# A two-layer decoder on one core: weighted values in pairs, a bank of their own for the small transposes, a mask of rank 32, and an earlier schedule for latents, routing and expert blocks

## The chip, the core and the metric

The kernel runs on one core of a Trainium2 chip. The metric is device microseconds of one execution, the median of several runs. Five engines work side by side, each in the order of its own program: TensorE (PE in the profile, its weight loads PEld), VectorE (DVE), ScalarE (ACT), GpSimd (POOL) and SyncE (SP, which here only issues DMAs). An engine whose next instruction waits holds everything behind it on that engine.

## The reference

Everything is float32. `x` holds 32 sequences of 128 tokens with 128 features; `ctx` holds 32 x 128 tokens with 96 features. Six residual steps follow one another:

```python
x = x + L0_attn(ln(x))         # 16 heads of 8, rotation by position, softmax over all keys
x = x + L0_xattn(ln(x), ctx)   # 16 heads of 8, keys and values from ctx, scores clipped
x = x + L0_ffn(ln(x))          # 8 gated experts of width 64, best 2 of 8, and 2 shared ones
x = x + L1_attn(ln(x))         # 16 heads of 8, rotation by head, causal mask
x = x + L1_xattn(ctx, ln(x))   # "latents": 2 heads of 64, 128 context keys and 128 own, mask, unit-norm q and k
x = x + L1_ffn(ln(x))          # 8 experts of width 512, best 2 of 8:

probs = softmax(xf @ router_w + router_b);  topk_w, topk_i = top_k(probs, 2)
gates[token, topk_i] = topk_w / sum(topk_w)
h = relu(xf @ w1[e] + b1[e]);  y = h @ w2[e] + b2[e];  out = sum_e gates[:, e] * y_e
```

## The kernel before

**Slots.** A group is four sequences (`NG`), so there are eight groups (`G`). The three attention stages (`rope`, `cross`, `causal`) of 32 sequences each make 96 batches. Each batch takes two slots, one for each half of the heads (`h` = 0 in even slots, 1 in odd ones): slots 0 to 63 are rope, 64 to 127 cross, 128 to 191 causal. `attention` keeps a table `plan` of functions by slot and phase. In each slot it runs, in this order: phase `open`, phase `pre`, the slot's own score work, phase `inner`, the weighted values, phase `mid`, phase `post` (L543 to L621). This order is the program order of every engine. There is no other scheduler. `done(stage, g)` is the slot in which a group has left a stage: 8(8 stage + g) + 17.

**The slot's own work.** For slot k, four matmuls on 32 rows of the array give the scores of batch k//2 (two banks of `ps_s`), in two row groups; in between stand eight matmuls on the other two row groups, which give the transposed scores of the slot five earlier (`LAG`; two banks of `ps_t`). Both are L584. In the causal stage two bf16 matmuls (L553) of the whole 128 x 128 array, with 512 columns each, add the mask to the two score banks first. Then VectorE takes the maxima (L587), and ScalarE the exponentials of the transposed scores into two tiles `e` (L595), which GpSimd cuts to the causal triangle (L598). The weighted values (L612, 128 rows by 32 columns of the array) follow for the slot six earlier, half a batch in each slot; after the odd one ScalarE copies the bank `av` (the only bank of `ps_a`) to `sums` (L618).

**The small transposes.** Two slots after a batch began, phase `post`, the maxima are transposed (`max_pe`, L485), and VectorE makes `qa` of them in phase `pre` of the next slot (`max_out`, L493). Eight slots after, phase `post`, `sums` is transposed (`sums_pe`, L500), and in phase `pre` of the next slot VectorE divides by the totals (`sums_out`, L510, L511). Each transposition takes a bank of `ps_m`, a ring of three that all other stages share.

**Beside it.** The other steps stand in the same slots. Group g's gated experts begin at `done(1, g)`. Its latents begin at d = `done(2, g)` + 2: statistics, scales on GpSimd (L1036 to L1044), `turn`, `qkv` (d+4, d+5), norms (`square`, `total`, `root` as a power on GpSimd, L1089, in d+5 and d+6, `unit_heads` on VectorE, L953 to L955, in d+6 and d+7, phase `mid`), then four batches, one begun every two slots from d+8, each of four steps (`turn`, `score`, `turn_e`, `weigh`), then `leave` (d+18) and `project` (d+19). The router works on units of one or two groups, `UNITS`; each step (`scale`, `apply`, `turned`, `choice`, `choose2`, `choose3`, `ranks`) has a slot. Then each token's row goes to its expert's place in DRAM by an indirect DMA that GpSimd issues (`scatter`, L1679, eight a group, two a slot). The experts run in two halves (groups 0 to 3, and 4 to 7) of 23 blocks of 256 rows, one block a slot: SyncE fetches weights (`fetch_w`, L1809, four buffers) and rows (`fetch_x`, L1818), `turn` transposes (L1826), `hidden` (L1836, L1844, L1846) and `result` (L1853, L1861, L1863) compute, and `leave` writes the rows to their tokens with two indirect DMAs on GpSimd (L1868). The rows stand in tile `bo`, four buffers. At the end the two rows of each token are read back and added (`gather`, `finish`, L1881 to L1886). `begins` sets the slots: 209 and 234 for the two halves.

**Start.** GpSimd makes the constants (identity, masks) before its first layer-norm scale; the warm-up matmuls (L284) wait for `ident_b`.

Of the kernel before, what the change touches and what calls it, by code (L numbers as in the profile page):

```python
# [22 lines left out]
P = 128  # L23
# [85 lines left out]
def decoder(ctx: ExitStack, tc: tile.TileContext, a: dict, out: bass.AP):  # L109
# [115 lines left out]
    causal = cpool.tile([P, P], F32, tag="causal", name="causal")  # L225
    make_causal_mask(nc, causal, CAUSAL)
    causal_b = cpool.tile([P, P], BF16, tag="causal_b", name="causal_b")
    nc.gpsimd.tensor_copy(causal_b, causal)
# [28 lines left out]
    def attention(att, rope, stages, besides):  # L257
# [36 lines left out]
        batch = [dict() for _ in range(B * len(stages))]  # L294
        half = {}
# [181 lines left out]
        def plan_batch(bb):  # L477
# [5 lines left out]
            def max_pe():  # L483
                s["mp"] = bank(ps_m)
                nc.tensor.transpose(s["mp"][:, :P], msc, ident)  # L485
                if st.guard:
                    nc.gpsimd.tensor_copy(m_all[:, bb % B], strided_max(msc))

            def max_out():
                s["qa"] = att.tile([P, 2, P], F32, tag="qa", name="qa", bufs=3)  # L490

                for u in range(2):
                    nc.vector.scalar_tensor_tensor(  # L493
                        s["qa"][:, u, :], s["mp"][:, :P], head_rows[:, 1 - u : 2 - u], m["qz"][:, u, i * P : (i + 1) * P], ALU.mult, ALU.add
                    )

            def sums_pe():
                s["tp"] = bank(ps_m)
# [19 lines left out]
            at(t + 2, "post", max_pe)  # L518
            at(t + 3, "pre", max_out)
            at(t + LAG + 3, "post", sums_pe)  # L520
# [22 lines left out]
        for k in range(-max(LEADS.values()), final + 1):  # L543
            run(k, "open")
            run(k, "pre")
            if 0 <= k < last:
# [4 lines left out]
                if st.causal:  # L551
                    for j in range(2):
                        nc.tensor.matmul(  # L553
                            sc[j].rearrange("p (n k) -> p n k", n=4), ident_b, wide(causal_b, [P, 4, P], 1),
                            start=True, stop=False, skip_group_check=True,
                        )
# [33 lines left out]
            if two:  # L590
                st2 = stages[bb2 // B]
                half[k2] = []
                for j in range(2):
                    e = att.tile([P, 4, P], F32, tag="e", name="e", bufs=4)
# [9 lines left out]
            if 0 <= k3 < last:  # L604
                bb3, h3 = divmod(k3, 2)
                m3, i3, s3 = made[bb3 // NG], bb3 % NG, batch[bb3]
                if h3 == 0:
                    s3["av"] = bank(ps_a)
                es = half.pop(k3)
                for u in range(2):  # L610
                    for n in range(4):
                        nc.tensor.matmul(  # L612
                            s3["av"][32 * n : 32 * n + 32, h3 * P : (h3 + 1) * P], m3["vt"][:, i3, h3, n, u, :], es[u][:, n, :],
                            start=(h3 == 0 and u == 0), stop=(u == 1), skip_group_check=True,
                        )
                if h3 == 1:
                    s3["sums"] = att.tile([P, 2 * P], F32, tag="sums", name="sums")
                    nc.scalar.copy(s3["sums"], s3["av"][:, : 2 * P])  # L618
# [389 lines left out]
    def latent_attention(lazy, kv, row, bias, masked, plan_route):  # L1008
# [3 lines left out]

        def opened():
# [7 lines left out]
        def plan_group(at, g, d):  # L1021
            m = {}
# [77 lines left out]
            for u in range(2):  # L1100
# [3 lines left out]
                at(d + 6 + u, "mid", lambda u=u: unit_heads(flat(u), n4, m["nrm", u]))  # L1104
            for i in range(NG):
                plan_batch(at, m, g, i, d + 8 + 2 * i)
# [15 lines left out]
            at(d + 18, "mid", leave)  # L1122
            at(d + 19, "mid", project)
            plan_route(at, g, d + 19)

        def plan_batch(at, m, g, i, t):
            b, s = g * NG + i, {}

            def fetch():
                s["kv"] = opened().tile([P, KV], F32, tag="kv", name="lkv", bufs=3)  # L1130
# [37 lines left out]
            def weigh():  # L1168
                if i == 0:
                    m["on"] = opened().tile([P, NG, D], F32, tag="on", name="lon", bufs=1)  # L1170
# [21 lines left out]
        def beside(at, done):  # L1192
            for g in range(G):
                plan_group(at, g, done(2, g) + LATER)
# [331 lines left out]
    UNITS = [(0, 1), (2, 3), (4, 5), (6,), (7,)]  # L1526
    HALVES = [(0, 1), (2, 3, 4)]

    def router(slots, lazy):
# [8 lines left out]
        def plan_route(at, g, t):  # L1538
# [203 lines left out]

            for u in us:
                at(t + 1 - 8 * (us[-1] - u), "mid", stats(u, 0))
                at(t + 2 - 8 * (us[-1] - u), "pre", stats(u, 2))
            at(t + 2, "mid", scale)
            for u in us:
                at(t + 3 + u, "mid", apply(u, 0))
                at(t + 4 + u, "pre", apply(u, 2))
                at(t + 4 + u, "mid", turned(u))  # L1750
            t += us[-1]
            at(t + 5, "mid", choice)
            at(t + 6, "mid", choose2)
            if len(groups) > 1:
                t += 1
            at(t + 6, "mid", choose3)
            at(t + 7, "mid", ranks)
            n = 0
            for k in range(n2):
                for c in range(2):  # L1760
                    at(t + 8 + n // 2, ("pre", "inner")[n % 2], scatter(c, k))
                    n += 1
            for u in us:
                at(t + 8 + u, "mid", gates_over(u))
                at(t + 9 + u, "mid", bias(u))
# [3 lines left out]
    def expert_blocks(f, total, lazy):  # L1769
# [5 lines left out]
        def table():  # L1775

            def row(shape, tag, dtype=F32):
                return lazy["blocks"].tile([1] + shape, dtype, tag="tb_" + tag, name="tb_" + tag, bufs=2 if tag == "where" else 1)
# [69 lines left out]
        def result(j):  # L1848
# [8 lines left out]
            o = s["o"] = lazy["blocks"].tile([P, 2, D], F32, tag="o", name="bo", bufs=4)  # L1857
# [32 lines left out]
    def experts(halves, lazy, heads, late):  # L1890

        def beside(at, done):
# [4 lines left out]
            at(done(2, G - 1) + 2, "open", swap)  # L1897
            begins = [done(2, G // 2 - 1) + 40, done(2, G - 1) + 33]

            def plan_half(f):  # L1900
# [3 lines left out]
                for j in range(3):  # L1904
                    at(t - 3 + j, "post", lambda j=j: fetch_w(j))
# [218 lines left out]
```

## Time and profile before

| what | value |
|---|---|
| time, median of 3 runs | 1189.68 us (1186.5 to 1194.54) |
| the profiled execution | 1213.03 us, span 1211.2 us |
| PE busy | 1107.3 us, 91% of the span |
| DVE, ACT, POOL busy | 808.4, 572.9, 632.4 us |
| causal mask on PE, L553 | 128 matmuls, 40.9 us busy |
| weighted values on PE, L612 | 3072 matmuls, 126.5 us busy |
| indirect DMAs on POOL, L1868 and L1679 | 92 and 64, 997 ns each |

The busy time of PE counts a matmul from its start to a modelled end, so neighbours overlap and a busy PE is not one at its peak. fp32 matmuls appear twice, once a pass. The maxima (L587, two a slot) show where the slots lie in time: the rope stage takes about 28 us for eight slots, cross about 39, causal about 42; the last score slot, 191, ends near 865 us. Slots 192 to 209 follow without expert blocks; the first block's transposition (L1826, slot 210) starts at 947 us, that of the second half's first block (slot 235) at 1095 us, and the last block's results leave at 1188 us. Of these stretches the windows further down give the engines' busy times and the granted clock.

### The profile page before, as it was taken

What the parts mean: (1) busy time and instruction counts of PE and PEld (TensorE: products, weight loads), DVE (VectorE), ACT (ScalarE), POOL (GpSimd) and SP (SyncE); (2) the same over time, 40 slices, a digit from 0 to 9 for tenths busy, and PEclk for the clock granted to TensorE, in tenths of its full rate; (3) what the DMA queues carried; (4) which work ended last, traced back from release to release, by engine and by line L of the source; (5) the groups of instructions that cost most, each with busy time, mean ns of one, the idle gap of its engine ahead of it and who ended that gap; (6) DMA issues with size and microseconds to landing.
All of it is one profiled execution on the core that took longest, in us unless ns stands there. A gap on an engine that the chain in (4) does not pass through costs nothing. (4 is left out here: it accounts for less than half of the span.)

```text
span 1211.2 us, 30676 instructions
## 1 busy us (share of the span) xinstructions
PE 1107.3 (91%) x11923; PEld 818.1 (68%) x11923; DVE 808.4 (67%) x2290; ACT 572.9 (47%) x1302; POOL 632.4 (52%) x905
## 2 busy tenths in 40 slices
PE   8999999999999999999999999989988898888991
PEld 3576776676666676656666666666666688777991
DVE  4688888777877877677667678768666564353441
ACT  2355556666655555554445655644553432322330
POOL 3654555344345335434637664746747356664663
PEclk8899999999999999999999999989987898898996
DMA  7705333101021100111020000000102244445873
GB/s 201 240 22 178 99 99 99 54 28 37 3 45 45 46 21 18 37 37 37 2 50 2 11 15 14 15 10 28 32 19 98 93 141 129 145 142 161 256 227 107
DMA packets 83081, 92.09 MB, mean 76 GB/s; under 512 B 14274, under 2 KB 70264, under 8 KB 82928
## 3 DMA queue, kind: packets, MB, share of 16 engines
q1 hardware_dynamic: 77936, 81.57, 23.1%
q0 software_dynamic: 4992, 8.48, 2.0%
q8 instruction: 96, 1.57, 0.5%
q14 instruction: 57, 0.47, 0.1%
HBM read 53.84 MB, written 38.01 MB: 76 GB/s over the span
## 5 line engine op out<-in xcount | busy, mean ns | idle before, releaser
L595 ACT ACTIVATE e<-bank 128x512 f32<-128x512 f32 x384 | 208.1, 595 | 221.6 <-PE bank L584 213.6
L587 DVE TENSOR_REDUCE msc<-bank 128x4 f32<-128x512 f32 x384 | 245.8, 681 | 68.5 <-PE bank L584 67.0
L584 PE MATMUL bank<-kb,qz 32*128 32x256 f32 x1536 | 237.5, 412 | 7.8 <-DVE msc L587 6.1
L584 PE MATMUL bank<-qa,kb 32*128 32x128 f32 x3072 | 233.4, 288 | 1.6 <-ACT e L595 1.6
L584 PEld LDWEIGHTS bank<-qa,kb 32*128 32x128 f32 x3072 | 194.7, 190 | 4.5 <-ACT e L595 3.5
L584 PEld LDWEIGHTS bank<-kb,qz 32*128 32x128 f32 x1536 | 141.9, 189 | 78.8 <-issue 42.2
L1868 POOL DMA_INDIRECT y<-bo,bx x92 | 91.7, 997 | 87.7 <-ACT bo L1861 65.8
L612 PE MATMUL bank<-e,vt 128*32 128x128 f32 x3072 | 126.5, 282 | 2.4 <-POOL e L598 2.4
L598 POOL TENSOR_SCALAR_AFFINE_SELECT e<-e 128x512 f32<-128x512 f32 x128 | 79.1, 642 | 94.4 <-ACT e L595 94.2
L1853 PE MATMUL bank<-w,bh 128*128 128x128 f32 x736 | 95.4, 285 | 1.0 <-issue 0.9
L1853 PEld LDWEIGHTS bank<-w,bh 128*128 128x128 f32 x736 | 92.7, 201 | 4.8 <-issue 3.3
L1836 PE MATMUL bank<-bxT,w 128*128 128x256 f32 x368 | 93.0, 396 | 2.7 <-DVE bh L1846 1.0
L612 PEld LDWEIGHTS bank<-e,vt 128*32 128x32 f32 x3072 | 73.0, 110 | 27.8 <-POOL e L598 3.9
L1679 POOL DMA_INDIRECT slots<-rows,r_ati x64 | 63.8, 997 | 32.6 <-issue 16.5
L1836 PEld LDWEIGHTS bank<-bxT,w 128*128 128x128 f32 x368 | 69.9, 201 | 13.2 <-issue 2.0
L891 POOL TENSOR_TENSOR h<-h,g 128x512 f32<-128x512 f32 x30 | 37.6, 1271 | 71.5 <-DVE nm_st L798 44.8
L1846 DVE TENSOR_SCALAR bh<-bank,w 128x256 f32<-128x256 f32 x92 | 40.2, 478 | 43.9 <-PE bank L1836 35.1
L1861 ACT ACTIVATE bo<-bank,bx 128x128 f32<-128x128 f32 x46 | 16.9, 367 | 96.8 <-PE bank L1853 56.5
L323 ACT ACTIVATE xn<-x,ln_nb,ln_rs 128x128 f32<-128x128 f32 x96 | 42.1, 494 | 41.0 <-POOL ln_nb L317 41.0
L493 DVE SCALAR_TENSOR_TENSOR qa<-bank,head_rows,qz 128x128 f32<-128x128 f32 x192 | 57.6, 342 | 2.2 <-PE bank L485 2.2
L1844 ACT ACTIVATE bh<-bank,w 128x256 f32<-128x256 f32 x92 | 38.6, 471 | 40.1 <-PE bank L1836 15.1
L1157 ACT ACTIVATE le<-bank,lmx 128x256 f32<-128x256 f32 x64 | 26.9, 471 | 64.1 <-DVE lmx L1156 56.7
(322 smaller groups left out, 2280.9 us busy)
## 6 DMA issues: line engine op xcount, KB each, us to landing
w<-in_w_f SPq DMA_DIRECT2D x46, 514.0 KB
slots<-nowhere SPq DMA_DIRECT2D x8, 2340.0 KB
g<-spread SPq DMA_DIRECT2D x16, 512.0 KB
bx<-slots SPq DMA_DIRECT2D x46, 130.0 KB
kv<-kcv SPq DMA_DIRECT2D x8, 516.0 KB
lkv<-kv SPq DMA_DIRECT2D x32, 129.0 KB
y<-y SPq DMA_DIRECT2D x16, 256.0 KB
x<-in_x SPq DMA_DIRECT2D x8, 256.0 KB
```

The costliest lines, as they stand in the source:

```text
L323: nc.scalar.activation(m["xn"][:, i, :], X[g][:, i, :], AF.Identity, scale=m["rs"][:, i : i + 1], bias=m["nb"][:, i : i + 1])
L493: nc.vector.scalar_tensor_tensor(s["qa"][:, u, :], s["mp"][:, :P], head_rows[:, 1 - u : 2 - u], m["qz"][:, u, i * P : (i + 1) * P], ALU.mu ...
L584: nc.tensor.matmul(o, l, r, start=start, stop=stop, skip_group_check=True)
L587: nc.vector.tensor_reduce(tops(MSC[bb % 4], 2 * h + j), sc[j].rearrange("p (s n k) -> p s n k", s=2, n=2), AX.X, ALU.max, negate=True)
L595: nc.scalar.activation(e.rearrange("p n q -> p (n q)"), tr[j], AF.Exp, scale=SCALE)
L598: nc.gpsimd.affine_select(out=e, in_=e, compare_op=ALU.is_ge, fill=0.0, base=0, pattern=[[0, 4], [1, P]], channel_multiplier=-1)
L612: nc.tensor.matmul(s3["av"][32 * n : 32 * n + 32, h3 * P : (h3 + 1) * P], m3["vt"][:, i3, h3, n, u, :], es[u][:, n, :], start=(h3 == 0 and ...
L1679: ins = nc.gpsimd.indirect_dma_start(slots[f], bass.IndirectOffsetOnAxis(ap=m["ati"][:, c, n : n + 1], axis=0), m["rows"][c][:, n, :], Non ...
L1836: nc.tensor.matmul(ps[:, c * BLOCK : (c + 1) * BLOCK], s["w"][:, (2 * k + c) * P : (2 * k + c + 1) * P], s["xT"], start=True, stop=True,)
L1846: nc.vector.tensor_scalar(s["h"][:, n, :], p, bias, 0.0, ALU.add, ALU.max)
L1853: nc.tensor.matmul(ps[:, u * P : (u + 1) * P], s["h"][:, c, u * P : (u + 1) * P], s["w"][:, 512 + c * P : 512 + (c + 1) * P], start=(c == ...
L1868: ins = nc.gpsimd.indirect_dma_start(y, bass.IndirectOffsetOnAxis(ap=s["x"][:, u, D : D + 1].bitcast(U32), axis=0), s["o"][:, u, :], None, ...
```

## The change

1. **Weighted values in pairs.** Both halves of a batch now run together in the odd slot, 32 instructions in one go; the even slot has none. Tile `e` gets 6 buffers for 4.
2. **The transposes in their bank.** `max_pe` and `sums_pe` share one bank of `ps_a` and move from phase `post` to a new phase `turn`, ahead of `mid`, in the same (even) slot.
3. **The mask of rank 32.** Eight matmuls on 32 rows (128 columns each), in the row groups of the slot's scores, replace the two on 128 rows.
4. **Shorter chain.** `unit_heads` moves from `mid` to `pre` of its slot; the latents' batches begin at d+6, and for the last group at one slot's distance, with d two earlier. The router's steps stand half a slot apart; `UNITS` splits (4, 5). `lkv` gets 6 buffers for 3, `lon` 2 for 1.
5. **Sooner blocks.** `begins` becomes 203 and 226; the first half's weights are fetched one slot ahead; the small tables come from pool `route`; `bo` gets 6 buffers for 4.

```diff
+    causal_b = cpool.tile([P, 4, P], BF16, tag="causal_b", name="causal_b")
+    nc.gpsimd.memset(causal_b, 0.0)
+    ident_32 = cpool.tile([P, 32], BF16, tag="ident_32", name="ident_32")
+    for r in range(0, P, 32):
+        nc.gpsimd.affine_select(
+            out=causal_b[r : r + 32], in_=causal_b[r : r + 32], compare_op=ALU.is_ge, fill=CAUSAL, base=0,
+            pattern=[[-32, 4], [1, P]], channel_multiplier=-1,
+        )
+        nc.gpsimd.tensor_copy(ident_32[r : r + 32], ident[r : r + 32, r : r + 32])
...
             def max_pe():
-                s["mp"] = bank(ps_m)
-                nc.tensor.transpose(s["mp"][:, :P], msc, ident)
+                if t + 2 not in shared:
+                    shared[t + 2] = bank(ps_a)
+                s["mp"] = shared[t + 2][:, 2 * P : 3 * P]
+                nc.tensor.transpose(s["mp"], msc, ident)
...
             def sums_pe():
-                s["tp"] = bank(ps_m)
+                s["tp"] = shared[t + LAG + 3] = bank(ps_a)
...
-            at(t + 2, "post", max_pe)
+            at(t + LAG + 3, "turn", sums_pe)
+            at(t + 2, "turn", max_pe)
             at(t + 3, "pre", max_out)
-            at(t + LAG + 3, "post", sums_pe)
...
                 if st.causal:
-                    for j in range(2):
-                        nc.tensor.matmul(
-                            sc[j].rearrange("p (n k) -> p n k", n=4), ident_b, wide(causal_b, [P, 4, P], 1),
-                            start=True, stop=False, skip_group_check=True,
-                        )
+                    for c in range(4):
+                        for j in range(2):
+                            rows = slice(64 * h + 32 * j, 64 * h + 32 * j + 32)
+                            nc.tensor.matmul(
+                                sc[j].rearrange("p (n k) -> p n k", n=4)[:, :, 32 * c : 32 * c + 32], causal_b[rows, c, :],
+                                wide(ident_32[rows], [32, 4, 32], 1), start=(c == 0), stop=False, skip_group_check=True,
+                            )
...
-            if 0 <= k3 < last:
+            if 0 <= k3 < last and k3 % 2 == 1:
...
+                for h3 in range(2):
+                    es = half.pop(k3 - 1 + h3)
...
+            run(k, "turn")
...
+        steps = [2] * (G - 1) + [1]
...
-                at(d + 6 + u, "mid", lambda u=u: unit_heads(flat(u), n4, m["nrm", u]))
+                at(d + 6 + u, "pre", lambda u=u: unit_heads(flat(u), n4, m["nrm", u]))
             for i in range(NG):
-                plan_batch(at, m, g, i, d + 8 + 2 * i)
+                plan_batch(at, m, g, i, d + 6 + step * i)
...
-            at(d + 18, "mid", leave)
-            at(d + 19, "mid", project)
-            plan_route(at, g, d + 19)
+            end = d + 6 + step * (NG - 1) + 4
+            at(end, "mid", leave)
+            at(end + 1, "mid", project)
+            plan_route(at, g, end + 1)
...
-                plan_group(at, g, done(2, g) + LATER)
+                plan_group(at, g, done(2, g) + (LATER if steps[g] > 1 else 0))
...
-    UNITS = [(0, 1), (2, 3), (4, 5), (6,), (7,)]
-    HALVES = [(0, 1), (2, 3, 4)]
+    UNITS = [(0, 1), (2, 3), (4,), (5,), (6,), (7,)]
+    HALVES = [(0, 1), (2, 3, 4, 5)]
...
+            steps.append(scale)
+            for u in us:
+                steps += [apply(u, 0), apply(u, 2)]
+            steps += [turned(u) for u in us]
+            steps += [choice, choose2, choose3, ranks]
+            for n, fn in enumerate(steps):
+                at(t + 1 + (n + 1) // 2, ("mid", "pre")[n % 2], fn)
+            t += 1 + (len(steps) + 1) // 2
...
-            o = s["o"] = lazy["blocks"].tile([P, 2, D], F32, tag="o", name="bo", bufs=4)
+            o = s["o"] = lazy["blocks"].tile([P, 2, D], F32, tag="o", name="bo", bufs=6)
...
-            at(done(2, G - 1) + 2, "open", swap)
-            begins = [done(2, G // 2 - 1) + 40, done(2, G - 1) + 33]
+            at(done(2, G - 1) + 1, "open", swap)
+            begins = [done(2, G - 1) + 2, done(2, G - 1) + 2 + NB]
...
-                    at(t - 3 + j, "post", lambda j=j: fetch_w(j))
+                    at(t - 3 + j if f else t - 1, "post", lambda j=j: fetch_w(j))
```

## The prediction

> **What bounds the kernel now.** I read the page first, then busy time by stretch (rope, cross, causal, the slots after them, the first half's blocks, the change of halves, the second half's blocks, the end), then the groups by line, and the timelines of PE and DVE where a wait ended.
>
> ```profile
> core 0: us, PE busy (x) PEld busy (x) DVE busy (x) ACT busy (x) POOL busy (x), PEclk, DMA share, GB/s
> 25.00:275.00 250.00, 239.95 (x3233) 170.12 (x3231) 195.70 (x534) 135.70 (x300) 128.07 (x179) 0.97 0.34 105
> 275.00:526.00 251.00, 238.79 (x2970) 170.10 (x2970) 186.99 (x521) 141.02 (x298) 106.08 (x179) 0.99 0.13 30
> 526.00:865.00 339.00, 317.31 (x3681) 218.42 (x3681) 244.71 (x662) 177.11 (x409) 197.09 (x294) 0.97 0.09 22
> 865.00:947.00 82.00, 72.07 (x534) 52.03 (x532) 54.80 (x184) 39.91 (x105) 50.39 (x70) 0.87 0.19 58
> 947.00:1076.00 129.00, 119.09 (x775) 105.83 (x774) 67.07 (x242) 39.19 (x99) 70.39 (x86) 0.91 0.41 133
> 1076.00:1095.00 19.00, 11.23 (x74) 9.33 (x72) 4.42 (x11) 3.51 (x9) 11.89 (x13) 0.94 0.37 115
> 1095.00:1188.00 93.00, 89.40 (x598) 83.25 (x598) 38.67 (x97) 28.14 (x70) 52.69 (x51) 0.96 0.65 203
> ```
>
> In the three attention stages PE is busy 94 to 96%, DVE 72 to 78%: PE's order sets the pace, and DVE is near enough to stop it. From 865 to 1095 us PE is still busy, but at a clock of 0.87 to 0.94, and much of that is waiting in small pieces. In 1095 to 1188 it is full: 23 blocks, starting every 3.73 us. Nothing there changes.
>
> ```profile
> L612 PE MATMUL bank<-e,vt 128*32 128x128 f32 x3072 | 126.5, 282 | 2.4 <-POOL e L598 2.4
> L553 PE MATMUL bank<-causal_b,ident_b 128*128 128x512 bf16 x128 | 40.9, 395 | 1.4 <-DVE msc L587 1.3
> L485 PE MATMUL bank<-ident,msc 128*128 128x128 f32 x96 | 29.7, 309 | 16.9 <-DVE h L885 9.5 <-ACT le L1157 5.4 <-DVE h L886 1.9
> L500 PE MATMUL bank<-ident,sums 128*128 128x128 f32 x192 | 39.2, 286 | 3.2 <-ACT le L1157 2.2 <-DVE lon L1182 0.9
> ```
>
> The small transposes wait 16.9 and 3.2 us for a bank of the ring of three, held by a gated expert's tanh product or by the latents' exponential. One slot and one wait:
>
> ```profile
> 121.14 0.64 PE L612 MATMUL bank<-e,vt 128*32 128x128 f32 x16
> 121.71 0.44 PE L500 MATMUL bank<-ident,sums 128*128 128x128 f32 x2
> ...
> 700.72 0.33 PE L485 MATMUL bank<-ident,msc 128*128 128x128 f32 x1 [0.65 <-ACT le L1157]
> 700.89 0.59 PE L553 MATMUL bank<-causal_b,ident_b 128*128 128x512 bf16 x2
> 701.41 0.48 PE L584 MATMUL bank<-kb,qz 32*128 32x256 f32 x2
> ```
>
> Sixteen instructions of L612 hold PE 0.57 us from start to next start; the mask pair 0.52 us.
>
> **The change part by part** (signed us on the profiled execution's 1213.0, which lies 23 above the median; minus is gained).
>
> *Pairs, -17.* The starts of L612's sixteen lie 24 ns apart (0.64 us less one's 0.28, by 15), so 0.37 us, and 0.20 more pass before the next instruction. Two separate sets take 1.14 us, 32 in one go 31 x 0.024 + 0.20 = 0.95. 96 batches x 0.18 = 17.
>
> *Own bank, -20.* The 16.9 + 3.2 us above have no cause left: `ps_a` is emptied by the copy L618 a slot earlier. The ring's next user comes at least a score set (1.1 us) later.
>
> *The new wait, +24.* The paired L612 takes `ps_a` over from the transposes, so in every odd slot it waits until VectorE has done `max_out` and `sums_out` of that slot, and these stand behind all that VectorE has left of the slot before. Queued behind L612 is all of PE's `mid` and `post`. In the trace of before I laid each odd slot's start of L612 against the end of L493 and L511 in that slot: where these end later, the differences sum to 19 us in rope, 12 in cross, 10 in causal, 41 in all. The longest comes once in eight rope slots, 2.4 us:
>
> ```profile
> 123.74 0.64 PE L612 MATMUL bank<-e,vt 128*32 128x128 f32 x16
> 124.32 1.16 PE L441 MATMUL bank<-w_v,xT 128*128 128x128 f32 x8
> ```
> ```profile
> 124.02 0.17 DVE L953 TENSOR_SCALAR nrmc<-nrmc 128x8 f32<-128x8 f32 x1 [1.42 <-POOL nrmc L999]
> ...
> 125.56 0.60 DVE L493 SCALAR_TENSOR_TENSOR qa<-bank,head_rows,qz 128x128 f32<-128x128 f32 x2
> ```
>
> VectorE waits 1.42 us for a power on GpSimd, and `qa` is done at 126.16, after L612's 123.74. Part comes back: the next score set waits for the maxima anyway (about 1.1 us there). I take 60%, 24; bounds 0 and 41.
>
> *Mask, -10.* Per slot 0.52 us become eight matmuls of 128 columns in two row groups. The nearest row is L1145, two bf16 matmuls of 32 rows and 128 columns in one row group, whose starts lie 0.07 us apart, weights included. With the two groups side by side, four steps of 0.07, and 0.09 for the change of array shape that now stands ahead of the mask and not behind it: 0.37, so -0.15 x 64 = -10. A rule speaks against it: the Trainium skill, "TensorE: Matmul & The Clock Gate", Part 3, says that a weight load overlaps running matmuls only if it goes to another row group, and its section on LDWEIGHTS makes a load of 128 columns P/1.2, 107 ns. Then each group's step is 107 + 53 (128 columns at 2.4 GHz) = 0.16, the slot 0.64 + 0.09, and the mask would cost +13. The row shows 0.07 for a load and a matmul in one group, so I go by it. Bounds: L612's pace of 24 ns each (-15), the rule (+13).
>
> *`unit_heads` in `pre`, +10.* It now stands ahead of the maxima. In five groups the power of the second half (L1089) ends 1.8 us after the maxima of that slot began (group 0: 661.58 against 659.78), and the work itself is 1.3 us (0.30 + 0.20 + 0.83). VectorE blocks, the next score set is late by what PE's `mid` does not cover: 2 us a group, 10; bounds 0 and 16. It leaves `mid`, where it made one of the waits above.
>
> *Start, +3.* GpSimd cuts `causal_b` in four pieces of 512 columns ahead of `ident_b` and of its first scale. L598, the same shape, takes 0.64 us: 2.5 more, and copies. Warm-up and the first scale (5.49 us) move with it. Bounds 0 and 4.
>
> *Slots 192 to first block, -22.* 865 to 947 is 19 slots of 4.3 us, in which no engine is full: they are as long as their chains. Now 13, with more in each (latents of the last group one a slot): I take 4.6, 60 us for 82. Bounds -30 and 0.
>
> *First half's blocks to the second's, 0.* 947 to 1095 holds 25 slots and, in whole pieces, 119 us of PE work (23 x 3.73, the rest latents and routing); the same work, 120, falls into 23 slots. Removed: the stop at the change of halves,
>
> ```profile
> 1095.26 0.66 PE L1826 MATMUL bank<-ident,bx 128*128 128x128 f32 x2 [5.25 <-DMA bx<-slots]
> ```
>
> two blocks in 19 us, 11 too many, because rows are fetched after the last scatter. SyncE now also stands behind its third weight fetch, whose buffer (four) is freed by `result` of block 21 in slot 227, one slot after the row fetches were due: 4 remain, -7. And waits for a free `bo`:
>
> ```profile
> 1035.88 0.37 ACT L1861 ACTIVATE bo<-bank,bx 128x128 f32<-128x128 f32 x1 [5.20 <-remote]
> ```
>
> four of them, 22.5 us on ACT; L1853 right after runs at half clock (3.57 us for 1.79). Six buffers bear two more slots of lag: -6, though I can't see that every such wait is a buffer's. Added: with steps half a slot apart PE meets `turned` and `ranks` before POOL, ACT and DVE are done. A chain choose3 and gates is 2.6 us of VectorE against some 2 of PE: 3 us for each of three units, +9. In slots 217 to 223 GpSimd issues two scatters and two results a slot, 4 x 1.28 = 5.1 us against 3.7 to 5 of PE: it falls behind by some 7 us and takes 4 from PE, +4.
>
> *At no cost:* the sixth unit adds about 25 VectorE instructions of 0.2 us and one GpSimd power (1.05 us); VectorE is busy 67 of 129 us there and covers them, else 6 us. SyncE's fetches of context keys stand two slots earlier and its first three weight fetches one slot earlier each; it issues one in 0.9 us and has slots of 4 us. Buffers and the pool of the tables cost no instruction.
>
> Sum: -17 - 20 + 24 - 10 + 10 + 3 - 22 + 0 = -32, 1181 profiled, in the same proportion **1158** for the median.
>
> **The rivals.**
>
> *Slower: GpSimd behind its slots holds the router and PE with it.* Place: slots 205 to 223. `scale` is queued on GpSimd after results and scatters; `turned` on PE follows 1.5 slots later (two before) and nothing on PE passes it. From a lag of about 4 us on, each of three units stops PE for the rest (up to 12 us) and half clock for 3 more: +45, 1158 + 45 = 1203. For it: 65.8 us of POOL's waits are for `bo`, so it cannot run ahead; scatters of two units meet in slot 220. Against: POOL is busy 70 of 129 us.
>
> *The gain of the tail alone, or of attention alone, is returned.* If DVE's waits come back not at all (+17) and the mask serializes (+23), attention gives nothing, and with a tail of -10 the time is near 1185.
>
> *Better than forecast:* with DVE's waits absorbed (-24) and the mask at 24 ns (-5) 1130. That the mask's row groups do not run side by side, so that part 3 is no saving, is the +23 above.
>
> **How the numbers follow.** Forecast (1135 to 1177): 0.48. Absorbed waits (below 1135): 0.12. Gains returned (1178 to 1201): 0.18. Slower, by GpSimd: 0.22, half of it above 1210. One per cent is about what a measurement of this kernel tells from no change. So faster 0.60, same 0.18, slower 0.22; the range 1115 to 1210 leaves out the far half of the slower case and a little below.
>
> **What would show it.** Right: L485 and L500 without idle time; L612 with an idle time released by L493 or L511, about 24 us; the mask under 0.4 us a slot; the first L1826 some 30 us earlier or more; no idle of 5 us before the second half's. Wrong: mask starts 0.16 us apart; PE idle before L1591 or L1651 of over 4 us, released by POOL's `r_nb` or by the picks on DVE; halved clock through the first half's blocks.

## The result and the profile after

The changed kernel takes 1267.85 us (median of 4 runs, 1266.46 to 1272.2), the kernel before 1189.49 us beside it: ratio 1.066, interval 1.0616 to 1.0705. Forecast was 1158. It is slower by 78 us, more than any of the rivals had it.

The profiled execution of the kernel before that the prediction was worked on lay 23 us above its median. A second profile of it took 1191.86 us and differs only behind slot 191 (320.6 us for 341.1 up to the last addition on VectorE; the stages before agree within 1.2 us). So the losses are read here between that profile and one of the changed kernel on the same chip (1269.18 us). The stages are cut at the end of the second maximum on VectorE in slots 0, 64, 128 and 191, at the first block's transposes, and at the last addition on VectorE:

| us | before | changed | difference | forecast |
|---|---|---|---|---|
| start to slot 0 | 22.5 | 25.6 | +3.1 | +3 |
| rope | 224.2 | 248.8 | +24.6 | attention in all: -13 |
| cross | 279.6 | 300.0 | +20.4 | |
| causal | 338.6 | 351.1 | +12.5 | |
| slot 191 to the first block | 79.6 | 88.6 | +9.0 | -22 |
| first block to the end | 241.0 | 248.2 | +7.2 | 0 |

The page's groups of the changed kernel (lines have moved: L612 is L623 now, L485 is L494, L500 is L509, L493 is L502, the mask is L564; after the bar: busy us, mean ns of one, idle before it and what ended that):

```profile
L623 PE MATMUL bank<-e,vt 128*32 128x128 f32 x3072 | 118.0, 299 | 92.1 <-DVE qa L502 85.7 <-DVE on L520 2.2 <-POOL x L359 1.6
L509 PE MATMUL bank<-ident,sums 128*128 128x128 f32 x192 | 42.5, 304 | 0.0
L564 PE MATMUL bank<-ident,causal_b 32*128 32x128 bf16 x512 | 28.8, 223 | 12.9 <-DVE msc L598 12.7
L494 PE MATMUL bank<-ident,msc 128*128 128x128 f32 x96 | 26.4, 275 | 0.0
```

Two forecasts stand there: the small transposes have no idle time (16.9 and 3.2 us before), and the mask waits 12.7 us for maxima that stand behind `unit_heads` (+10 forecast). But L623 waits 92.1 us where L612 waited 2.4: 27 in rope, 35 in cross, 28 in causal, 2 behind. One of these waits, first on PE, then on DVE:

```profile
128.99 0.39 PE L595 MATMUL bank<-qa,kb 32*128 32x128 f32 x4
131.86 1.94 PE L623 MATMUL bank<-e,vt 128*32 128x128 f32 x32 [2.48 <-DVE qa L502]
```
```profile
126.90 1.26 DVE L598 TENSOR_REDUCE msc<-bank 128x4 f32<-128x512 f32 x2
129.57 0.17 DVE L964 TENSOR_SCALAR nrmc<-nrmc 128x8 f32<-128x8 f32 x1 [1.42 <-POOL nrmc L1010]
...
130.01 0.69 DVE L966 TENSOR_TENSOR kc<-kc,nrmc 128x512 f32<-128x512 f32 x1
130.62 0.25 DVE L519 RECIPROCAL rz<-bank 128x16 f32<-128x16 f32 x1
130.91 0.29 DVE L520 TENSOR_TENSOR on<-bank,rz 128x128 f32<-128x128 f32 x1
131.11 0.60 DVE L502 SCALAR_TENSOR_TENSOR qa<-bank,head_rows,qz 128x128 f32<-128x128 f32 x2
```

The bank's last reader, `qa`, ends at 131.71; VectorE came to it only after a power on GpSimd and a whole `unit_heads`, and L623 starts right behind. PE also comes back at half pace: these 32 matmuls take 1.94 us, those of an undisturbed slot 1.08; 21 of the 96 sets are slowed.

Busy time by stretch in the changed kernel (the columns after the engines: granted TensorE clock, DMA share, GB/s):

```profile
26.00:272.00 246.00, 213.81 (x2842) 159.84 (x2841) 175.60 (x474) 120.70 (x260) 116.50 (x158) 0.92 0.33 101
272.00:572.00 300.00, 263.48 (x3355) 194.26 (x3356) 205.18 (x583) 162.25 (x337) 116.67 (x200) 0.97 0.12 28
572.00:923.00 351.00, 303.38 (x4080) 230.61 (x4082) 242.87 (x676) 183.25 (x416) 201.23 (x300) 0.94 0.09 23
923.00:1012.00 89.00, 74.99 (x518) 58.39 (x508) 50.41 (x183) 33.59 (x86) 49.13 (x70) 0.71 0.16 48
```

Rope, cross and causal hold the same work as before but stretch, and their clock fell from 0.97, 0.99 and 0.97. Behind slot 191 there are 13 slots for 19, yet 89 us for 80, at 0.71 for 0.87.

### The profile page after: what moved, and what is told of

Its sections match the earlier page's. It is cut to its first block, busy times and chain, and to the rows that moved or that the text cites. A ratio compares the mean times of both kernels' runs of the same rounds, so it can differ in the third digit from the quotient of the medians.

```text
span 1265.1 us, 31429 instructions
## 1 busy us (share of the span) xinstructions
PE 1087.7 (86%) x12309; PEld 846.6 (67%) x12309; DVE 806.2 (64%) x2323; ACT 584.3 (46%) x1303; POOL 637.0 (50%) x917
## 4 chain that ended last, share of the span: by engine, by line
PE 48%; DVE 26%; POOL 11%; issue 8%; ACT 4%; DMA 2%; POOLq 0%; SPq 0%; DVEq 0%; ACTq 0%
PE bank L623 8%; PE bank L595 8%; DVE msc L598 4%; POOL y L1881 3%; PE bank L911 3%; DVE qa L502 3%; PE bank L378 2%; PE bank L1866 2%; PE bank L893 2%; PE bank L1849 2%; DVE h L897 2%; DVE on L520 2%; DVE h L896 2%; PE bank L415 2%; PE bank L1084 1%
## 5 line engine op out<-in xcount | busy, mean ns | idle before, releaser
L595 PE MATMUL bank<-qa,kb 32*128 32x128 f32 x3072 | 236.8, 293 | 1.8 <-ACT e L606 1.8
L595 PEld LDWEIGHTS bank<-qa,kb 32*128 32x128 f32 x3072 | 198.4, 195 | 4.2 <-ACT e L606 2.9
L623 PE MATMUL bank<-e,vt 128*32 128x128 f32 x3072 | 118.0, 299 | 92.1 <-DVE qa L502 85.7
L595 PEld LDWEIGHTS bank<-kb,qz 32*128 32x128 f32 x1536 | 145.8, 192 | 55.1 <-issue 22.4
L623 PEld LDWEIGHTS bank<-e,vt 128*32 128x32 f32 x3072 | 90.4, 119 | 110.1 <-issue 52.5
L1866 PE MATMUL bank<-w,bh 128*128 128x128 f32 x736 | 92.1, 280 | 0.0
L1849 PE MATMUL bank<-bxT,w 128*128 128x256 f32 x368 | 90.3, 390 | 0.2 <-DMA w<-in_w_f 0.2
L628 ACT COPY sums<-bank 128x256 f32<-128x256 f32 x96 | 35.8, 373 | 85.3 <-PE bank L623 85.0
L502 DVE SCALAR_TENSOR_TENSOR qa<-bank,head_rows,qz 128x128 f32<-128x128 f32 x192 | 57.6, 342 | 0.0
```

Of the source, the lines that this page charges most:

```text
L502: nc.vector.scalar_tensor_tensor(s["qa"][:, u, :], s["mp"], head_rows[:, 1 - u : 2 - u], m["qz"][:, u, i * P : (i + 1) * P], ALU.mult, ALU.add
L595: nc.tensor.matmul(o, l, r, start=start, stop=stop, skip_group_check=True)
L623: nc.tensor.matmul(s3["av"][32 * n : 32 * n + 32, h3 * P : (h3 + 1) * P], m3["vt"][:, i3, h3, n, u, :], es[u][:, n, :], start=(h3 == 0 and ...
L1849: nc.tensor.matmul(ps[:, c * BLOCK : (c + 1) * BLOCK], s["w"][:, (2 * k + c) * P : (2 * k + c + 1) * P], s["xT"], start=True, stop=True,)
L1866: nc.tensor.matmul(ps[:, u * P : (u + 1) * P], s["h"][:, c, u * P : (u + 1) * P], s["w"][:, 512 + c * P : 512 + (c + 1) * P], start=(c == ...
```

## The experiments

Twelve runs, two of them of the two kernels once more; every ratio is against the kernel before on the same chip (1214.24 us for the first four, about 1195 for the others). Attention's three stages agree in the two profiles of the kernel before: 224.3, 278.4 and 339.5 us in the one, 224.2, 279.6 and 338.6 in the other. The chips differ behind slot 191, as experiments 5 and 6 tell. Of most edits only a part is shown; `...` marks what is left out.

**1. The hand-over taken away.** The bank goes from the transposes, over their readers on VectorE, to the paired L623: this is called the hand-over below. Here the readers stand right behind the transposes, in the same slot (early reads), so that the bank is free long before L623.

```diff
-            at(t + 3, "pre", max_out)
-            at(t + LAG + 4, "pre", sums_out)
+            at(t + 2, "turned", max_out)
+            at(t + LAG + 3, "turned", sums_out)
...
             run(k, "turn")
+            run(k, "turned")
```

> The changed kernel, with the reads of the transposed maxima and sums put in the even slot right behind the transposes, ahead of that slot's other work, so that the bank is free before the paired L623 of the odd slot asks for it. Theory A (the single bank that goes from the transposes through VectorE to the paired weighted values is what costs): L623's idle time falls from 92 us to under 20, PE's clock rises again, and the time falls from 1267 to about 1190. Rival B (the pairing itself, or the moved order, costs): L623 still idles, or the same idle shows up ahead of another row, and the time stays above 1240. Rival C (the latents and the blocks cost): attention gets faster in the trace, but the time stays above 1230, with the loss in the slots after 191.

Measured: 1228.63 us, ratio 1.0121 (1.0091 to 1.0151). Its group of the paired matmuls:

```profile
L623 PE MATMUL bank<-e,vt 128*32 128x128 f32 x3072 | 109.7, 286 | 0.4 <-POOL e L609 0.4
```

The wait is gone whole. Rope, cross and causal are 220.3, 274.5 and 336.9 us, 66 less than in the changed kernel's first profile (68 less than in the table): of 92 us of waiting 72% were lost time. Theory A holds for attention. But 1.2% above before is left, although the gains are now free of the wait: there is a second loss.

**2. Pairs alone.** The changed kernel's loop over `k3` and its buffers for `e`, and nothing else:

```diff
-            if 0 <= k3 < last:
+            if 0 <= k3 < last and k3 % 2 == 1:
...
-                    e = att.tile([P, 4, P], F32, tag="e", name="e", bufs=4)
+                    e = att.tile([P, 4, P], F32, tag="e", name="e", bufs=6)
```

> The kernel before with the weighted values in pairs alone (the small transposes stay in their ring of three, six buffers for e). Theory A: no new wait, since the bank of the weighted values is emptied by ScalarE's copy alone; 96 batches of 0.18 us are saved, so -10 to -17 us, about 1175. Rival B (32 matmuls in one go, or their place a slot later, is what hurts): slower than before by 20 us or more, with idle time ahead of L484-L500's transposes or the score set.

Measured: 1217.52 us, ratio 1.0017 (0.9992 to 1.0041): neither. The 32 matmuls are not slow (L612's busy sum falls from 126.5 to 105.3 us), but the 17 us do not come out:

```profile
L612 PE MATMUL bank<-e,vt 128*32 128x128 f32 x3072 | 105.3, 278 | 0.0
...
L485 PE MATMUL bank<-ident,msc 128*128 128x128 f32 x96 | 29.9, 311 | 28.9 <-DVE h L883 17.6 <-ACT le L1155 4.5 <-DVE h L884 2.9
```

PE arrives sooner at the next thing that is late: the wait for the ring's bank grows from 16.9 to 28.9 us. Alone, the pairs do not pay.

**3. The mask alone.** Setup and matmuls of the rank-32 mask on the kernel before:

```diff
...
-                            sc[j].rearrange("p (n k) -> p n k", n=4), ident_b, wide(causal_b, [P, 4, P], 1),
...
+                                sc[j].rearrange("p (n k) -> p n k", n=4)[:, :, 32 * c : 32 * c + 32], causal_b[rows, c, :],
...
```

> The kernel before with the mask of rank 32 alone. From the changed kernel's trace, where mask and scores together take 1.25 us a slot instead of 1.62: 64 slots by 0.37 is -24 us at most, and as the score set also waits for VectorE's maxima, -10 to -24 is expected. If a weight load did not run beside matmuls of its own row group the mask would take 0.73 us a slot for 0.52: +13. The three stages without a mask must not move by more than a microsecond or two, but for the start (+3).

Measured: 1205.17 us, ratio 0.9935 (0.9912 to 0.9959). Causal takes 328.4 us for 339.5, the start 2.4 more, rope and cross some 1.2 less each. One slot's mask (L560) and scores (L591), up to the next line:

```profile
700.50 0.34 PE L560 MATMUL bank<-ident,causal_b 32*128 32x128 bf16 x6
700.64 0.38 PE L591 MATMUL bank<-qa,kb 32*128 32x128 f32 x2
700.68 0.22 PE L560 MATMUL bank<-ident,causal_b 32*128 32x128 bf16 x2
...
701.75 0.42 PE L619 MATMUL bank<-e,vt 128*32 128x128 f32 x7
```

1.25 us from the mask's start to L619, where the two wide matmuls and the scores of a slot took 1.63 in the kernel before: 0.38 by 64 slots is 24 us, of which 11 reach the time. Mask and scores run into one another, which no bound of mine had: in the median of the 64 slots the first score matmul starts 0.135 us behind the first of the mask.

**4. Latents, routing and blocks alone.** The changed kernel, less pairs, own bank and mask:

```diff
...
-            at(t + LAG + 3, "turn", sums_pe)
-            at(t + 2, "turn", max_pe)
+            at(t + 2, "post", max_pe)
             at(t + 3, "pre", max_out)
+            at(t + LAG + 3, "post", sums_pe)
...
```

> The kernel before with only the latents' and the router's parts of the change (one-slot steps in the last group, unit_heads ahead of the maxima, half-slot steps in the routing, six units, the first half's blocks after the last group's slots, more buffers). By the prediction: +10 for unit_heads, -22 and 0 for the slots after 191, so about -12, 1178. By the changed kernel's trace, where the stretch from slot 191 to the end took 342 us for 346: +6, 1195. Rival C (this part carries the loss): 1220 or more.

Measured: 1261.75 us, ratio 1.0369 (1.0332 to 1.0407): rival C. Against the first profile of the kernel before, causal is 24.5 us longer (364.0) and the stretch behind slot 191 another 24.5 (365.6).

**5 and 6. Both kernels once more.**

> The kernel before, profiled once more. Its profiled execution lay 23 us above the median of its runs, and in it TensorE's semaphore updates after 800 us are often some microseconds late. If that belongs to the execution and not to the kernel, a second profile has another stretch from slot 191 to the end than 341 us (by up to 23 us less), with the three attention stages within 2 us of 224, 278 and 340. If it belongs to the kernel, all stretches come out the same.

> The changed kernel again, beside its undone parts. In ratio to the kernel before it was 1.066. Adding up what the parts measured alone (latents and blocks +3.7%, mask -0.7%, pairs +0.2%, own bank -1.6% by its waits) leaves 1.016; with the hand-over of the bank (66 us from attention's three stages against the early-read kernel) 1.07. If the ratio is near 1.066 here too, the parts add up; if it is near 1.04, part of the loss is that of the chip or of the parts' meeting.

Measured: 1191.86 us in one run, with the shorter end told above, so the 20 us behind slot 191 do not belong to the kernel. Nor do they belong to a single execution, as the expectation had it: the kernel before took 1209 to 1221 us in all 31 runs on the chip of experiments 1 to 4, and the profiles from there show the same long end (experiment 3, which leaves that stretch as it was, has 346.0 us from slot 191 to the end of the span, the first profile of the kernel before 345.9, the second 325.2). It goes with the chip; which chip the first profile came from is not on record. The changed kernel: 1268.03 us, ratio 1.061 (1.0564 to 1.0655): near 1.066, so the parts add up, though the hand-over's 66 us were themselves taken from this kernel. Its stages are in the table.

**7. The attention parts alone, with early reads.** Pairs, own bank, mask and edit 1; latents, routing and blocks as before. Against experiment 1:

```diff
...
-                plan_batch(at, m, g, i, d + 6 + step * i)
+                plan_batch(at, m, g, i, d + 8 + 2 * i)
...
-            begins = [done(2, G - 1) + 2, done(2, G - 1) + 2 + NB]
+            begins = [done(2, G // 2 - 1) + 40, done(2, G - 1) + 33]
...
```

> Pairs, own bank and mask on the kernel before, with the transposes read out in the slot in which they are made, and nothing of the latents, the routing and the blocks. Theory A with C (two losses: the hand-over of the bank, and the latents with the blocks): both are gone, so the kernel beats the one before by the mask (-9), the own bank (-17 to -20) and 0 for the pairs: about -26 us, ratio 0.978. If instead moving the transposes in front of mid costs something by itself, the ratio is 0.99 or more, with idle time ahead of the score set.

Measured: 1163.66 us, ratio 0.9744 (0.9702 to 0.9787). It beats both kernels, by 31 us and by 104. Rope, cross and causal are 220.3, 272.2 and 309.6 us, 40 less than before in all (my pairs, bank and mask: 47).

```profile
L622 PE MATMUL bank<-e,vt 128*32 128x128 f32 x3072 | 107.1, 280 | 1.8 <-POOL e L608 1.8
L508 PE MATMUL bank<-ident,sums 128*128 128x128 f32 x192 | 42.2, 302 | 0.0
L493 PE MATMUL bank<-ident,msc 128*128 128x128 f32 x96 | 26.4, 275 | 0.0
```

The matmuls hardly wait here, the transposes not at all. Behind slot 191 it gives 5.7 us back (326.3 for 320.6), and the start, with the new mask's constants, 3.4.

**8. `unit_heads` back in `mid`**, in the kernel of experiment 1.

```diff
-                at(d + 6 + u, "pre", lambda u=u: unit_heads(flat(u), n4, m["nrm", u]))
+                at(d + 6 + u, "mid", lambda u=u: unit_heads(flat(u), n4, m["nrm", u]))
```

> The changed kernel with early reads, and unit_heads back in mid, behind the maxima. In the early-read kernel the mask L564 waited 14.7 us in causal for VectorE's maxima. If unit_heads ahead of them is what causal lost (my +10), 10 to 15 us of its ratio of 1.012 go, to about 1.00; if those waits only move to the batches' first matmul L1085 and L1160, which need its result, it stays at 1.01.

Measured: 1204.49 us, ratio 1.0096 (1.0053 to 1.0138). Causal is 334.2 us for 336.9. The mask's wait shrinks, and the transposes of `lqk` (L1151) wait 11.5 us in causal instead of 2.7: the wait only moved. With the batches at `d + 6` it makes no difference clear of noise where in its slot `unit_heads` stands.

**9. The latents' steps closer, alone,** on the kernel of experiment 7. Two moves in one: `unit_heads` to `pre`, and the batches two slots earlier.

```diff
-                at(d + 6 + u, "mid", lambda u=u: unit_heads(flat(u), n4, m["nrm", u]))
+                at(d + 6 + u, "pre", lambda u=u: unit_heads(flat(u), n4, m["nrm", u]))
             for i in range(NG):
-                plan_batch(at, m, g, i, d + 8 + 2 * i)
+                plan_batch(at, m, g, i, d + 6 + 2 * i)
```

The group's end follows two slots earlier, and the context's buffers are the changed kernel's.

> The attention-only kernel (0.974 of before) with the latents' steps two slots closer (unit_heads in pre, batches from d + 6, end earlier), two slots a batch in every group, nothing else of routing and blocks. Theory C1 (the steps now stand closer than they take, and PE, in order, stops in each): causal 15 to 25 us longer than the attention-only kernel's 310, PE idle ahead of the batches' first transposes and L1157's masked products, granted clock in the slots from 160 on down from 1.00 to about 0.91; ratio about 0.99. Theory C2 (it is the routing): causal within 3 us of 310.

Measured: 1207.02 us, ratio 1.0108 (1.0081 to 1.0134), 3.6% above experiment 7 (a ratio of about 0.99 was expected); causal 341.0 us for 309.6, and 11 us more behind slot 191. This is the second loss; of its two moves the first alone was not tried, but experiment 8 took it back and gained nothing that can be told. VectorE in one slot of a group, first of experiment 7, then of this one:

```profile
711.62 0.68 DVE L958 TENSOR_REDUCE nrml<-lsq 128x8 f32<-128x512 f32 x1
712.21 0.68 DVE L476 TENSOR_TENSOR x<-bank,x 128x512 f32<-128x512 f32 x1
713.41 1.29 DVE L597 TENSOR_REDUCE msc<-bank 128x4 f32<-128x512 f32 x2 [0.52 <-PE bank L594]
715.45 0.69 DVE L1177 COPY leT<-bank 128x512 f32<-128x512 f32 x1 [0.75 <-PE bank L1175]
716.06 0.16 DVE L964 TENSOR_SCALAR nrml<-nrml 128x8 f32<-128x8 f32 x1
```
```profile
728.89 0.68 DVE L958 TENSOR_REDUCE nrml<-lsq 128x8 f32<-128x512 f32 x1
729.49 0.68 DVE L476 TENSOR_TENSOR x<-bank,x 128x512 f32<-128x512 f32 x1
731.36 0.17 DVE L964 TENSOR_SCALAR nrml<-nrml 128x8 f32<-128x8 f32 x1 [1.19 <-POOL nrml L1102]
731.57 0.20 DVE L965 RECIPROCAL nrml<-nrml 128x8 f32<-128x8 f32 x1
731.81 0.91 DVE L966 TENSOR_TENSOR lqk<-lqk,nrml 128x512 f32<-128x512 f32 x1
732.64 1.27 DVE L597 TENSOR_REDUCE msc<-bank 128x4 f32<-128x512 f32 x2
```

The sum of squares goes to GpSimd for a power of 1.67 us. In experiment 7 the maxima L597 start 1.79 us behind the sum, and the power's reader L964 comes after them without a wait. Here L964 stands first, waits 1.19 us, and the maxima start 3.75 us behind the sum; the next scores wait for them. Two such slots a group, and the batches' transposes and products in the same slots: a group of eight slots takes 46.2 and 44.1 us for 37.4 each. And the clock, for three groups (first experiment 7, then this one):

```profile
671.00:708.00 37.00, 35.65 (x527) 27.71 (x526) 31.91 (x90) 23.84 (x60) 23.86 (x37) 1.00 0.07 16
708.00:745.00 37.00, 35.64 (x527) 27.68 (x527) 31.85 (x91) 23.83 (x60) 24.15 (x37) 1.00 0.06 16
745.00:793.00 48.00, 42.85 (x574) 33.65 (x573) 38.67 (x116) 28.09 (x69) 27.85 (x44) 0.96 0.05 14
```
```profile
679.00:725.00 46.00, 39.78 (x529) 30.30 (x528) 31.89 (x91) 24.63 (x60) 24.69 (x37) 0.93 0.05 13
725.00:769.00 44.00, 37.93 (x525) 28.83 (x524) 31.99 (x91) 25.17 (x62) 27.45 (x42) 0.96 0.05 14
769.00:827.00 58.00, 50.14 (x591) 38.71 (x592) 38.37 (x117) 29.36 (x70) 30.20 (x44) 0.88 0.06 17
```

The same work (527 and 529 matmuls in the trace) keeps PE busy 39.8 us for 35.7. In causal the trace has the clock at half for 41.0 us, for 13.7 in experiment 7, though no stop of PE there is longer than 3.1 us in either. So the loss (31 us in causal) is twice the added idle time (35.9 us of gaps over 0.15 us for 21.5); the other half is slower matmuls.

**10. The routing alone,** half-slot steps and six units, on the kernel of experiment 7:

```diff
-    UNITS = [(0, 1), (2, 3), (4, 5), (6,), (7,)]
+    UNITS = [(0, 1), (2, 3), (4,), (5,), (6,), (7,)]
...
+                at(t + 1 + (n + 1) // 2, ("mid", "pre")[n % 2], fn)
```

> The attention-only kernel with the routing's half-slot steps and six units alone, blocks where they were. Theory C2: causal 15 us or more longer and PE idle ahead of r_both and rows of 5 us or more; ratio 0.985 to 0.99. Theory C1: causal within 3 us of the attention-only kernel's 310, and my prediction's +9 for the units spread over the slots from 160; ratio about 0.975 to 0.98.

Measured: 1172.35 us, ratio 0.9819 (0.9736 to 0.9902), about 9 us above experiment 7, though the two intervals overlap. Causal is 310.6 us (309.6), slot 191 to the first block 101.4 (86.9), from there to the end 231.1 (239.3).

**11. Latents and routing,** all of the change but the sooner blocks, with early reads. Against experiment 1:

```diff
...
-            begins = [done(2, G - 1) + 2, done(2, G - 1) + 2 + NB]
+            begins = [done(2, G // 2 - 1) + 40, done(2, G - 1) + 33]
...
```

> The attention-only kernel with the latents' and the routing's parts as in the changed kernel (last group one slot a batch too), and the blocks where they were. What is left to the early-read kernel is the sooner first half's blocks. If the blocks' place brings what I predicted (-22 for the slots after 191), this kernel is some 20 us slower than the early-read kernel's ratio of about 1.012; if the blocks' place brings nothing, it is at 1.00 to 1.01; if it costs, below 1.00.

Measured: 1210.17 us, ratio 1.0155 (1.0073 to 1.0238). The kernel of experiment 1, which has the sooner blocks too, was at 1.0121 (1.0091 to 1.0151). What the blocks' place brings lies within what these two can't tell apart; 20 us it is not.

**12. Routing, and one slot a batch in the last group alone** (its d two slots earlier, as in the change), at the old distance of two slots behind the norms:

```diff
+        steps = [2] * (G - 1) + [1]
...
-                plan_batch(at, m, g, i, d + 8 + 2 * i)
+                plan_batch(at, m, g, i, d + 8 + step * i)
```

> The attention-only kernel with the routing's half-slot steps, and one slot a batch in the last group alone, with the batches two slots behind the square roots and unit_heads in mid as before. A faster version if the shortened chain of the last group brings anything: the second half's rows come some slots earlier, its wait (about 9 us of the 14 at the change of halves) shrinks: ratio 0.965 to 0.975. If the chain is bound by the time of its steps and not by slots: no better than the attention-only kernel, 0.974 or more.

Measured: 1174.66 us, ratio 0.9828 (0.9746 to 0.9911), as experiment 10: the last group's shorter chain brings nothing that these runs can tell (the interval is 1.6% wide), and not the 0.965 to 0.975 of the case in which it pays. From slot 191 to the first block it takes 105.3 us: the steps' time, not the number of slots, seems to set that stretch.

## Why the prediction was wrong

*Pairs, -17, and own bank, -20.* The transposes' waits went as forecast. The pairs alone brought 0: the shorter PE work only brings PE sooner to a wait. They also save less than I took: a pair holds PE 1.01 us from start to next start, two halves 1.15, so 13 us and not 17. Together with the mask, and with early reads, 40 of 47 us came; how they share in it was not tried.

*The new wait, +24: the first step that failed.* The mechanism was right, with its place and even its example, but it cost 66 us, from 92 of idle time, and even that cost is above my upper bound of 41. The bound laid DVE's ends against the old starts of L612 as if these would stay. They don't: the pairs take the even slot's sixteen matmuls, 0.57 us, from in front of each of those starts. Laying them again in the same trace, batch by batch, gives 41 us with the old starts and 84 with starts 0.57 us earlier. That is worked out, not tried. It comes near the 92 in sum, but less so by stage (36, 27 and 20 us in rope, cross and causal, for 27, 35 and 28), so why the wait is just this long stays open in part. The sum booked the pairs' gain in full and the wait as if there were no pairs. And I took 60% of the idle time as lost; it was 72%: against experiment 1, PE's idle time in the three stages is 57 us longer, 62% of the 92, and its busy time 9, for matmuls slowed behind the stops.

*Mask, -10.* Near in time: -11 in causal, -9 in the median. The rule that spoke against it (the Trainium skill, "TensorE: Matmul & The Clock Gate", Part 3: a weight load overlaps running matmuls only if it goes to another row group) is not what happens here. My estimate from it was 0.16 us a step and +13; in experiment 3 the mask's matmuls of one row group, each with its own load, start 0.056 to 0.066 us apart (medians of the 64 slots), and mask and scores together take 0.38 less than before.

*`unit_heads` in `pre`, +10.* The mask's wait of 12.7 us, 11 more than before, has the size that I had worked out, and experiment 8 shows that with the batches at `d + 6` leaving it in `mid` saves nothing clear of noise. What it costs with the batches at `d + 8` was not tried.

*What the sum left out: the second step that failed.* The change also moves every group's batches from `d + 8` to `d + 6`, and so takes away the two slots that stood between `unit_heads` and its readers. I read that move as a gain for the last group (inside *Slots 192 to first block, -22*) and put no price on it in the other groups, that is in causal. Experiment 9 puts it, together with `unit_heads` in `pre`, at 3.6%, some 43 us, 31 of it in causal; 10 of them stood in my sum, so some 33 were missing. The rule of my own working, that every step that is moved counts with its chain, was kept for the routing and not for the latents.

*Slots 192 to first block, -22.* It became +9. I took 4.6 us for each of 13 slots; they take 6.8. The chain of steps behind one another is as long as before, as I read it, and now it stands in fewer slots, in each of which PE stops. The waits of PE in the changed kernel from slot 191 on (us in all, times, longest):

```profile
PE bank L1084 <- DVE lon L1196: 4.5, 1, 4.5
PE bank L1665 <- DVE r_both L1650: 4.3, 3, 2.1
PE bank L1159 <- DVE lon L1196: 2.9, 1, 2.9
PE bank L1159 <- DVE x L1727: 2.8, 1, 2.8
```

Few and short, but between them PE runs at a clock of 0.71. The experiments with the old 19 slots there say the same: 86.9 us in experiment 7, but 105.0, 101.4 and 105.3 in experiments 9, 10 and 12, and 123.5 in experiment 11. More steps to a slot make the slot longer.

*First half's blocks, 0.* +7 from the first block to the end. Two of its terms did not come. The stop ahead of the second half's first block, which was to shrink by 7, is still there: 4.4 us of idle time on PE for 5.0. And the waits ahead of L1861 that I gave to a missing `bo` buffer (-6) were not the kernel's: its second profile, with the same four buffers, has no wait for an unknown releaser.

*The rivals.* GpSimd behind its slots was not the cause: L1665, where it would have stopped PE, waits 4.3 us behind slot 191, in three pieces of at most 2.1, for VectorE. That the gains are returned was the nearest. Its 1185 was summed wrongly: +17 and +23 turn attention's -13 into +27, and with the start's +3 and a tail of -10 that makes 1209 for the median. The measured time lies above that too.

So the 78 us are: -31 for the attention parts with free reads (0.974), +58 to +64 for the hand-over, +43 for the latents' closer steps and some +9 for the routing (its interval is wide), and nothing that can be told for the blocks: 79 to 85 in all, against 78 and 73 measured. The hand-over is the difference between the changed kernel and experiment 1, so what this tests is the rest: 21, against 14 for experiment 1 and 18 for experiment 11.

## What to carry to other kernels

When a change shortens the work in front of a wait, shift the old start times before laying them against the other engine; a bound taken from unshifted times is no bound. Price every moved step by the chain between its producer and its reader, in each stage where it occurs: slots between them that look empty may be what hides a round trip through two other engines. And a bank that passes from one engine's readers to the next writer wants its readers placed right behind its producer.

## What was not expected of the hardware

Mask and score matmuls of different row groups run into one another: eight loads with their matmuls and the whole score set in 1.25 us. And PE ran at half clock for 41.0 us of one stage in which no stop was longer than 3.1 us (experiment 9).

In the profile of experiment 1, on the chip where the kernel before took 1214 us, readers started long after the matmuls that they read had ended by the profile's modelled ends. First PE's rows, then VectorE's that read what these wrote:

```profile
986.78 1.89 PE L1850 MATMUL bank<-bxT,w 128*128 128x256 f32 x8
988.61 1.16 PE L1720 MATMUL bank<-b,rgT 8*128 8x128 f32 x8
```
```profile
993.83 0.88 DVE L1860 TENSOR_SCALAR bh<-bank,w 128x256 f32<-128x256 f32 x2 [4.67 <-remote]
996.70 0.69 DVE L1728 TENSOR_TENSOR x<-bank,x 128x512 f32<-128x512 f32 x1 [1.99 <-remote]
```

L1850 ends at 988.67 and its reader starts at 993.83; L1720 ends at 989.77 and its reader starts at 996.70. ScalarE's reader of L1850's other bank started at 990.96: the three lie 2.87 us apart. GpSimd issued indirect transfers without a pause meanwhile. Waits for an unknown releaser (`remote`) come to 31 us in the first profile of the kernel before (22.5 of them ahead of L1861, of which the prediction showed one) and to 25 to 29 us in the four profiles of experiments 1 to 4, these four from that chip. The nine other profiles have none at all. So this goes with the chip and not with a kernel, as far as these profiles tell, and it fits the 20 us by which that chip is slower. What causes it was not tried.
